# Graph attention turned round: scores with keys on partitions, a multiplied mask, no maximum, and the sum as a 33rd column

## The chip, the cores and the metric

The kernel runs on one core of a Trainium2 chip. The metric is the device time of that core in microseconds (us); lower is better. The kernel before took 2525.3 us, the median of 3 runs (2523.89 to 2526.6).

## The reference

128 graphs of 64 nodes with 256 features go through four layers, each with a layer norm and a ReLU ahead of it and a residual sum behind it. Layers 0 and 1, which the change touches, are attention with 8 heads of 32 features inside each graph. Layer 0 masks by the adjacency, layer 1 adds its logarithm. Layer 2 is a gated graph network with five steps, layer 3 a gated graph convolution. Everything is float32.

```python
# layer 0
q, k, v = split_heads(h @ Wq + bq), split_heads(h @ Wk + bk), split_heads(h @ Wv + bv)
scores = einsum('bhqd,bhkd->bhqk', q, k) / sqrt(HD)
scores = where(adj[:, None] > 0, scores, NEG)
attn = softmax(scores, axis=-1)
out = einsum('bhqk,bhkd->bhqd', attn, v) ... @ Wo + bo
# layer 1
scores = einsum('bhqd,bhkd->bhqk', q, k) / sqrt(HEAD_DIM)
scores = scores + log(adjacency + 1e-06)[:, None]
attn = softmax(scores, axis=-1)
# layer 2: for each of five steps
m = h @ weight[l];  agg = einsum('bij,bid->bjd', A, m);  h = gru_cell(agg, h, ...)
# layer 3
f_hom = norm * (adj @ ((h @ theta) * norm));  f_het = h @ W_h
out = elu(gate * f_hom + (1 - gate) * f_het)          # gate = sigmoid(h @ W_t + b_t)
```

## The kernel before

The program is written out in full, without loops on the chip. Two graphs make a pair of 128 tokens, four pairs a group; there are 16 groups. `attend` works on half a group (two pairs, 256 tokens) in one layer, so it runs 16 x 2 x 2 = 64 times. The order of instructions on each engine is worked out ahead by a planner in the kernel's own Python, which interleaves the groups: while one group is in the five steps of layer 2, the next is in attention and the one before in layer 3. The planner knows costs of operations, among them a cost of changing the shape of the TensorE tiles (full array, 64 by 64, 64 by 32, transposes), and constants such as `FRONT` and `BACK_SPAN` that say how the groups overlap.

The scores come with queries on partitions. DVE scales and biases them, takes the maximum over keys and subtracts it; ACT takes the exponential; DVE sums and inverts; POOL multiplies by the inverse; TensorE turns the weights (`aT`) so that keys lie on partitions; ACT copies them; and in the next call TensorE weighs V.

```python
def scores():                                  # 16 matmuls, tiles of 64 x 64
    for i in range(2):
        for c in range(2):
            for gp in range(2):
                for rh in range(2):
                    ...
                    nc.tensor.matmul(ps[gp * NODES : (gp + 1) * NODES, 2 * c : 2 * c + 2, i, :],
                                     qk[s, c, gp, 0, i * NODES : (i + 1) * NODES],
                                     k_exp[s, c, :, t0 : t0 + NODES], start=True, stop=True)
...
if waiting:                                    # the weighing of the call before, then these scores
    _, weigh_last, reads, po_last, oT_last, finish_last = waiting.pop()
    pe(655, weigh_last, reads, po_last, holds=[oT_last], mode=T32)
    pe(860, scores, [qk, k_exp], pss, holds=es, mode=T64)
    finish_last()
...
for i in range(2):                             # the softmax, twice 128 x 512
    vec(...)   # L767 scalar_tensor_tensor: e = ps * scale + bias
    vec(...)   # L772 tensor_reduce max
    vec2(...)  # L774 e - max
    sca(...)   # L776 exp
    vec(...)   # L777 tensor_reduce sum
    vec(...)   # L779 reciprocal
    pool(...)  # L780 e * (1 / sum)
    def turn(e=e, pa=pa):
        for h in range(4):
            nc.tensor.transpose(pa[:, h * P : (h + 1) * P], e[:, h, :], ident.tile)   # L786
    pe(437, turn, [e, ident], [pa], holds=[aT], mode=TURN)
    sca(...)   # L790 aT <- pa
...
def weigh():                                   # 32 matmuls, tiles of 64 x 32, 64 columns moving
    ...
    nc.tensor.matmul(o[q * HD : (q + 1) * HD, c, s], v[rows, gp, h * HD : (h + 1) * HD],
                     aTs[q // 2][rows, 2 * c + q % 2, s], start=True, stop=True)     # L805

def finish():
    # L813: two copies of 128 x 256, oT <- po;  L818: four matmuls y = oT @ Wo;  L821: x = y + x
    ...

CHANGE = ((0, 95, 95, 0), (250, 30, 135, 200), (237, 135, 30, 187), (0, 95, 95, 0))  # ns, planner
```

Of the kernel before, what the change touches and what calls it, by code (L numbers as in the profile page):

```python
# [11 lines left out]
ALU = mybir.AluOpType  # L12
# [47 lines left out]
FRONT = 0.1  # L60
FRONT_LAST = 0.25
FRONT_SPAN = 0.95
BACK = -0.1
BACK_LAST = 0.35
BACK_SPAN = 0.65
STEP = 0.0
STEP_LAST = -0.1
STEP_SPAN = 0.5
LOCK = 0.3
BACK_END = 0.1  # L70
ENTRY = -0.05
FIRST = -1.2
FIRST_SPAN = 1.2
ORDER = (0, 0, 1, 0, 1, 0)
FUSE = -1.1
FUSE_SPAN = 0.25

# [192 lines left out]

@with_exitstack
def gnn_stack_kernel(ctx: ExitStack, tc: tile.TileContext, a: dict, out: bass.AP):
    nc = tc.nc
    x, adj, nodemask = a["x"], a["adj"], a["nodemask"]
# [95 lines left out]
    with plan.strand(-3.0, 0.1):  # L370


        few = new("few", [P, 7 + PAIRS], 1)

        def fill(n, key, value, rows=slice(0, P)):
            pool(60, lambda: nc.gpsimd.memset(few[rows, n], value), [], [(few, key)])

        fill(slice(0, 1), 0, 1e-6)
        fill(slice(1, 1 + PAIRS), 1, -0.5)
        parity, k_bias = PAIRS + 1, PAIRS + 3  # L380
        fill(slice(parity, parity + 2), 2, 0.0)
        for q in range(4):
            fill(slice(parity + q % 2, parity + q % 2 + 1), 2, 1.0, slice(q * HD, (q + 1) * HD))
        ident = new("ident", [P, P], 1)
        pool(600, lambda: make_identity(nc, ident.tile), [], [ident])

        warm = bank("warm")

        def turn_ident():
            for _ in range(20):  # L390
                nc.tensor.transpose(warm[:, :P], ident.tile, ident.tile)

        pe(4000, turn_ident, [ident], [warm])


        n_rows = 18 + n_pairs
        rows = new("f", [n_rows, P], 1, "rows")

        def fill_rows():
            r0 = 0  # L400
            for name in ("L0_gnn_bq", "L0_gnn_bk", "L2_gnn_b_ih", "L2_gnn_b_hh", "L0_gnn_bv"):
                n = a[name].shape[0] // P
                nc.scalar.dma_start(rows.tile[r0 : r0 + n, :], a[name].rearrange("(r p) -> r p", p=P))
                r0 += n
            nc.scalar.dma_start(rows.tile[r0 : r0 + n_pairs, :],
                                nodemask.rearrange("(t a) n -> t (a n)", a=2))

        plan.add("ACT", 2600, fill_rows, [], [rows], lat=6200)
        load_x(0)

        first = [new("h", [P, 2, 2, D], 4, f"w_{n}") for n in ("qk0", "qk1", "v")]

        def load_first(layer, i):
            t, j = (first[layer], i) if i < 2 else (first[2], layer)
            dma(256, lambda: nc.sync.dma_start(
                t[:, j], a[f"L{layer}_gnn_W{'qkv'[i]}"].rearrange("(c p) o -> p c o", p=P)), [], [(t, j)])
            return t, j

        of_first = [[load_first(0, i) for i in range(2)], []]
        load_adj(0)  # L420

        gw = []

        def load_gw(l):
            t = new(("sg", "sg", "sn", "sn", "Th")[l], [P, 2, D], 2 if l < 4 else 1, f"gw_{l}")
            dma(256, lambda: nc.sync.dma_start(
                t.tile, a["L2_gnn_weight"][l].rearrange("(c p) e -> p c e", p=P)), [], [t])
            gw.append(t)

        load_gw(0)  # L430
        of_first[0].append(load_first(0, 2))
        w_ih = []
        for c, tag in enumerate(("ht", "agg")):
            t = new(tag, [P, 3 * D], 2 if tag == "ht" else 1, f"w_ih{c}")
            dma(384, lambda c=c, t=t: nc.sync.dma_start(
                t.tile, a["L2_gnn_w_ih"][c * P : (c + 1) * P, :]), [], [t])
            w_ih.append(t)
        attn = [(load_w("L0_gnn_Wo", D), load_row("L0_gnn_bo"))]
        for l in range(1, LAYERS):
            load_gw(l)  # L440
        load_x(1)
        of_first[1] = [load_first(1, i) for i in range(3)]
        attn.append((load_w("L1_gnn_Wo", D), load_row("L1_gnn_bo")))
        w_hh = new("w_hh", [P, 3, 7, P], 1)

        def load_hh():
            for c in range(2):
                nc.sync.dma_start(
                    w_hh[:, :, 2 * c : 2 * c + 2, :],
                    a["L2_gnn_w_hh"][c * P : (c + 1) * P, :].rearrange("p (g o q) -> p g o q", g=3, o=2))  # L450

        dma(768, load_hh, [], [w_hh])
# [13 lines left out]
    with plan.strand(-0.9, 0.1):  # L466

        w_o, bo = attn[0]
        bvb = new("aT", [P, 4, P], 2, "bvb")
        pbo = bank("bvo")  # L470
        for c in range(2):
            vec(200, lambda c=c: nc.vector.tensor_copy(
                bvb[:, c, :], cols[:, 16 + c : 17 + c].to_broadcast([P, P])), [cols], [(bvb, c)])
            pe(mm(256), lambda c=c, w_o=w_o: nc.tensor.matmul(
                pbo[:, :D], bvb[:, c, :], w_o[:, c, :], start=c == 0, stop=c == 1),
                [(bvb, c), w_o], [pbo])
        vec(dve(256), lambda bo=bo: nc.vector.tensor_tensor(bo.tile, pbo[:, :D], bo.tile, op=ALU.add),
            [pbo, bo], [bo])
# [25 lines left out]
    def power(dst, src, at, eps, n, name):  # L504

        s = new("pw", [P, n], 3, f"pw_{name}")
        vec2(70, lambda: nc.vector.tensor_scalar(s.tile, at(), eps, None, op0=ALU.add), [src], [s])  # L507
# [27 lines left out]
    def norm_relu_t(xt, half, dst, access, writes, name, by_token=None, by_graph=False):  # L535

        st = new("st", [P, 2, 6], 3, f"st_{name}")
        mv = new("mv", [P, 2, 2], 3, f"mv_{name}")
        rstd = new("rstd", [P, 2], 3, f"rstd_{name}")
        for i in range(2):  # L540
            p = 2 * half + i
            vec(332, lambda p=p, i=i: nc.vector.bn_stats(st[:, i, :], xt[:, p, :]), [(xt, p)], [(st, i)])
            vec(83, lambda i=i: nc.vector.bn_aggr(mv[:, i, :], st[:, i, :]), [(st, i)], [(mv, i)])
        power(rstd, mv, lambda: mv[:, :, 1], EPS, 2, name)
        xn = new("xn", [P, 2, D], 1, f"xn_{name}")
        for i in range(2):
            p = 2 * half + i
            vec2(325, lambda p=p, i=i: nc.vector.tensor_scalar(
                xn[:, i, :], xt[:, p, :], mv[:, i, 0:1], rstd[:, i : i + 1],
                op0=ALU.subtract, op1=ALU.mult), [(xt, p), mv, rstd], [(xn, i)])  # L550
# [53 lines left out]
    def attend(layer, xt, half, bias, bias_at, name, plain):  # L604
# [9 lines left out]
        v = new("v", [P, 2, D], 2, f"v_{name}")  # L614
# [15 lines left out]
        def plainly():  # L630
# [22 lines left out]
            for gp in range(2):  # L653
# [4 lines left out]
            sca(act(512), lambda: nc.scalar.activation(  # L658
                v.tile, pv.tile.rearrange("p (g f) -> p g f", g=2), AF.Copy), [pv], [v])

        def by_seven():
# [38 lines left out]
            def total(bk, t, c, gp):  # L700
# [3 lines left out]
                    v[:, gp, c * P : (c + 1) * P], bk[:, 2 * P : 3 * P], t[:, 2, :], op=ALU.add),  # L704
# [21 lines left out]
            sca(act(128), lambda: nc.scalar.activation(v[:, 0, P:], pb[:, 2 * P : 3 * P], AF.Copy), [pb], [(v, (1, 0))])  # L726
# [9 lines left out]
        def scores():  # L736
# [4 lines that stand above are left out]
# [3 lines left out]
                            nc.tensor.matmul(ps[gp * NODES : (gp + 1) * NODES, 2 * c : 2 * c + 2, i, :],  # L744
# [4 lines left out]
        es = [new("e", [P, 4, 2 * NODES], 3, f"e_{name}_{i}") for i in range(2)]  # L749
        if waiting:  # L750
            _, weigh_last, reads, po_last, oT_last, finish_last = waiting.pop()
            pe(655, weigh_last, reads, po_last, holds=[oT_last], mode=T32)
# [8 lines left out]
        aTs = []  # L761
        shape = [P, HEADS, NODES]
        for i in range(2):
            ps, e = pss[i], es[i]
            m = new("smax", [P, HEADS], 3, f"smax_{name}_{i}")
# [31 lines left out]
        def weigh():  # L797
            for gp in range(2):
                s = slice(gp * NODES, (gp + 1) * NODES)
                for c in range(2):  # L800
                    for q in range(4):
                        for i in range(2):
                            rows, h = slice(i * NODES, (i + 1) * NODES), 4 * c + q
                            o = po[i][:, :D].rearrange("p (c t) -> p c t", c=2)
# [4 lines left out]
        oT = new("oT", [P, 2, 2, P], 1, f"oT_{name}")  # L809

        def finish():
            for i in range(2):
                vec(dve(256), lambda i=i: nc.vector.tensor_copy(  # L813
                    oT[:, i], po[i][:, :D].rearrange("p (c t) -> p c t", c=2)), [po[i]], [(oT, i)])
            py = bank(f"y_{name}")
            for i in range(2):
# [4 lines left out]
            vec(dve(512), lambda: nc.vector.tensor_tensor(  # L821
                xt[:, pp : pp + 2, :], py.tile.rearrange("p (t d) -> p t d", t=2), xt[:, pp : pp + 2, :],
                op=ALU.add), [py, (xt, pp), (xt, pp + 1)], [(xt, pp), (xt, pp + 1)])

        waiting.append((xt, weigh, [v, *aTs], po, oT, finish))

    def flush(xt):
# [4 lines left out]
        pe(655, weigh, reads, po, holds=[oT], mode=T32)  # L832
# [321 lines left out]
    def front(g):  # L1154

        if g % ADJ_GROUPS == 0 and (g // ADJ_GROUPS + 1) * ADJ_GROUPS < n_groups:
# [5 lines left out]
        neg = new("neg", [P, PAIRS, NODES], 1, f"neg_{g}")  # L1162
        vec2(200, lambda: nc.vector.tensor_scalar(
            neg.tile, adjq[:, sel, :], 0.0, NEG, op0=ALU.is_le, op1=ALU.mult), [adjq], [neg])
        for layer in range(2):
            if layer and not g % ADJ_GROUPS:
                log_adj(g // ADJ_GROUPS)
            ladj = adj_vals[g // ADJ_GROUPS][1]
            for half in range(2):
                bias = ladj if layer else neg  # L1170
# [18 lines left out]
        power(norm, deg, lambda: deg.tile, 1e-6, PAIRS, f"deg_{g}")  # L1189
# [15 lines left out]
    def entry(g, xt):  # L1205
# [3 lines left out]
        for half in range(2):  # L1209
            norm_relu_t(xt, half, h, lambda half=half: h[:, :, half * HALF : (half + 1) * HALF],  # L1210
                        [(h, (0, half)), (h, (1, half))], f"{g}_2_{half}", ht)
# [162 lines left out]
    for at, g, l in events:  # L1374
# [19 lines left out]
        if l + 1 == LAYERS:  # L1394
            with plan.strand(begin[g] + 2 + BACK + (BACK_LAST if g + 2 == n_groups else BACK_END if last else 0), BACK_SPAN):
                back(g, *held.pop(g))
    plan.run()
# [33 lines left out]
```

## Time and profile before

| | |
|---|---|
| Time | 2525.3 us (3 runs, 2523.89 to 2526.6) |
| Span of the profiled execution | 2523.7 us, 58158 instructions |
| Granted TensorE clock | 0.998 |
| TensorE transposes of the weights (aT) | 512 records |
| TensorE scores / weighing | 2048 / 4096 records |
| DVE steps of the softmax, in groups of 128 | sum over keys 84.3 us, maximum 83.7 us, minus maximum 86.1 us |
| DMA | 188.47 MB, mean 75 GB/s |

The profile is one execution on the chip. A row of its groups of instructions gives line, engine, operation, tiles written and read, shapes and count; after the bar the time in which at least one instruction of the group ran (us) and the mean duration of one (ns); after the second bar the idle time of the engine just before them. Each matmul of float32 leaves two records, each transpose one. PE is TensorE, PEld its weight loads, DVE VectorE, ACT ScalarE, POOL GpSimd. Matmuls are pipelined, so the duration of one record is longer than the time from its start to the next start.

### The profile page before, as it was taken

The numbers are of one execution on the slowest core, as the hardware profiler recorded it, in microseconds if no ns is written. First come the engines' busy times: TensorE is split into PE (matmuls) and PEld (weight loads), VectorE is DVE, ScalarE is ACT, GpSimd is POOL, SyncE is SP. The second block draws the span as 40 slices with busy tenths as digits, with TensorE's granted clock in tenths as the row PEclk, the third lists the DMA queues.
The fourth block names the chain that finished last, engine by engine and source line by source line (L and its number), as shares of the span: only waits on it lengthen the run. The fifth ranks groups of instructions, "written<-read, shape, count | busy, mean of one in ns | idle before, by whom it ended". The sixth has DMA issues, their size and how long they took to land.

```text
span 2523.7 us, 58158 instructions
## 1 busy us (share of the span) xinstructions
PE 2501.1 (99%) x23511; PEld 2150.9 (85%) x23511; DVE 2038.7 (81%) x4632; ACT 1394.8 (55%) x2806; POOL 879.7 (35%) x892
## 2 busy tenths in 40 slices
PE   9999999999999999999999999999999999999998
PEld 7788888888888888888888888888888888888885
DVE  7886787887878888798877978878788887887667
ACT  4456555555556555565555655556555555555444
POOL 5632323424333333333423334243333333333121
PEclk9999999999999999999999999999999999999999
DMA  6511212113121122222113121131211222211120
GB/s 198 174 67 61 93 49 79 62 54 106 51 99 64 61 75 71 79 71 73 59 68 101 50 84 65 52 101 52 98 64 64 68 71 79 71 49 67 49 71 18
DMA packets 78256, 188.47 MB, mean 75 GB/s; under 512 B 14802, under 2 KB 66852, under 8 KB 67108
## 3 DMA queue, kind: packets, MB, share of 16 engines
q1 hardware_dynamic: 77872, 184.71, 21.8%
q8 instruction: 186, 3.05, 0.5%
q14 instruction: 82, 0.67, 0.1%
q10 hardware_dynamic: 116, 0.04, 0.0%
HBM read 166.70 MB, written 18.02 MB: 73 GB/s over the span
## 4 chain that ended last, share of the span: by engine, by line
PE 96%; DVE 3%; ACT 0%; issue 0%; POOL 0%; DMA 0%; DVEq 0%; POOLq 0%; ACTq 0%
PE gb L932 22%; PE gc L932 17%; PE nb L932 11%; PE nc L932 8%; PE qkvb L682 6%; PE qkvc L682 5%; PE y L818 4%; PE agg L972 3%; PE l3b L1254 3%; PE s L744 3%; PE lnT L522 2%; PE l3c L1254 2%; PE aT L786 2%; PE hT L522 2%; PE o L805 2%; PE hom L1321 1%
## 5 line engine op out<-in xcount | busy, mean ns | idle before, releaser
L1041 POOL TENSOR_TENSOR sn<-h,sn 128x512 f32<-128x512 f32 x158 | 209.1, 1327 | 464.1 <-ACT sn L1039 463.7
L508 POOL TENSOR_TENSOR rstd<-pw,few 128x2 f32<-128x2 f32 x128 | 101.6, 794 | 482.9 <-DVE pw L507 459.7
L780 POOL TENSOR_TENSOR e<-e,ssum 128x512 f32<-128x512 f32 x128 | 149.4, 1175 | 315.9 <-DVE ssum L779 284.5
L932 PE MATMUL gb<-Th,w_hh 128*128 128x256 f32 x960 | 248.1, 381 | 0.0
L932 PE MATMUL gb<-Ta,gv 128*128 128x256 f32 x960 | 246.5, 379 | 0.0
L901 POOL TENSOR_TENSOR Th<-h 128x256 f32<-128x256 f32 x160 | 129.5, 829 | 249.6 <-PE nb L932 177.0
L932 PEld LDWEIGHTS gb<-Th,w_hh 128*128 128x128 f32 x960 | 178.1, 190 | 28.6 <-POOL Th L901 0.4
L932 PEld LDWEIGHTS gb<-Ta,gv 128*128 128x128 f32 x960 | 179.6, 190 | 25.3
L1039 ACT ACTIVATE sn<-sn,b_n 128x512 f32<-128x512 f32 x158 | 114.2, 724 | 123.4 <-DVE sn L1037 121.6
L932 PE MATMUL gc<-h,w_hh 128*128 128x256 f32 x640 | 166.1, 382 | 0.1
L932 PE MATMUL gc<-agg,gv 128*128 128x256 f32 x640 | 165.6, 381 | 0.0
L1043 DVE SCALAR_TENSOR_TENSOR sn<-sg,sn 128x512 f32<-128x512 f32 x158 | 107.4, 686 | 58.5 <-POOL sn L1041 58.3
L1024 ACT ACTIVATE sg<-sg,b_rz 128x512 f32<-128x512 f32 x158 | 105.5, 714 | 78.5 <-DVE sg L1004 78.5
L932 PE MATMUL nb<-Th,w_hh 128*128 128x256 f32 x480 | 144.1, 382 | 0.0
L932 PE MATMUL nb<-Ta,gv 128*128 128x256 f32 x480 | 143.0, 380 | 0.0
L901 POOL TENSOR_TENSOR Th<-h,Th 128x256 f32<-128x256 f32 x160 | 139.1, 869 | 10.4 <-DVE h L1045 4.6
L818 PE MATMUL y<-w_L_gnn_Wo,oT 128*128 128x256 f32 x512 | 138.9, 382 | 0.0
L1035 DVE SCALAR_TENSOR_TENSOR sn<-sg,sn 128x512 f32<-128x512 f32 x158 | 110.4, 700 | 34.8 <-ACT sn L1146 31.7
L985 DVE TENSOR_TENSOR Ta<-agg 128x256 f32<-128x256 f32 x160 | 92.3, 588 | 51.5 <-PE nb L932 41.2
L932 PEld LDWEIGHTS gc<-agg,gv 128*128 128x128 f32 x640 | 118.4, 190 | 16.9 <-issue 2.5
L996 ACT ACTIVATE p5g<-gc 128x512 f32<-128x512 f32 x79 | 46.9, 594 | 149.5 <-PE gc L932 149.4
L932 PEld LDWEIGHTS gc<-h,w_hh 128*128 128x128 f32 x640 | 116.3, 190 | 15.5 <-ACT sg L1031 0.5
(224 smaller groups left out, 6943.4 us busy)
## 6 DMA issues: line engine op xcount, KB each, us to landing
gv<-gates SPq DMA_DIRECT2D x80, 1344.0 KB, 6.0
qw<-kept SPq DMA_DIRECT2D x203, 192.0 KB, 2.4
x<-in_x_dram SPq DMA_DIRECT2D x32, 256.0 KB, 5.5
out_dram<-x SPq DMA_DIRECT2D x32, 256.0 KB, 2.3
gates<-gv SPq DMA_DIRECT2D x5, 1344.0 KB, 5.3
adjq<-in_adj_dram SPq DMA_DIRECT2D x8, 256.0 KB, 4.2
gw<-in_L_gnn_weight_dram SPq DMA_DIRECT2D x5, 256.0 KB, 6.4
kept<-s SPq DMA_DIRECT2D x8, 128.0 KB, 3.5
```

Of the source, the lines that this page charges most:

```text
L508: pool(660 if n == 2 else 970, lambda: nc.gpsimd.tensor_tensor(dst.tile, s.tile, few[:, 1 : 1 + n], op=ALU.pow), [s, (few, 1)], [dst], port=2)
L682: nc.tensor.matmul(bk[:, j * P : (j + 1) * P], lhs, rhs, start=first and j == 0, stop=True, skip_group_check=True)
L780: pool(1000, lambda e8=e8, z=z: nc.gpsimd.tensor_tensor(e8(), e8(), z[:, :, None].to_broadcast(shape), op=ALU.mult), [e, z], [e])
L818: pe(mm(256), lambda i=i, c=c: nc.tensor.matmul(py[:, i * D : (i + 1) * D], oT[:, i, c, :], w_o[:, c, :], start=c == 0, stop=c == 1), [(oT ...
L901: pool(690, lambda: nc.gpsimd.tensor_tensor(T[:, i, :], x(), y(), op=ALU.subtract), reads, [(T, i)])
L932: nc.tensor.matmul(bank_[:, col * HALF : (col + 1) * HALF], at(g, n), rhs(), start=first and j == 0, stop=True, skip_group_check=True)
L1024: sca(act(TOK, 1.5), lambda k=k, col=col: nc.scalar.activation(g_v[:, :, k, :], g_v[:, :, k, :], AF.Tanh, bias=b_rz[:, col : col + 1], sca ...
L1035: vec2(dve(TOK), lambda: nc.vector.scalar_tensor_tensor(a_(), r(), 1.0, a_(), op0=ALU.add, op1=ALU.mult), [*ts[0], n_v], [n_v])
L1039: sca(act(TOK, 1.5), lambda: nc.scalar.activation(a_(), a_(), AF.Tanh, bias=b_n[:, oc : oc + 1]), [n_v, b_n], [n_v])
L1041: pool(1230, lambda: nc.gpsimd.tensor_tensor(b_(), hh(), a_(), op=ALU.subtract), [*hp, n_v], [n_v])
L1043: vec2(dve(TOK), lambda: nc.vector.scalar_tensor_tensor(b_(), z(), 1.0, b_(), op0=ALU.add, op1=ALU.mult), [*ts[1], n_v], [n_v])
L1254: pe(mm(384), lambda: nc.tensor.matmul(bk[:, : 3 * P], b(), w3[:, :, n, :], start=first, stop=True, skip_group_check=True), [w3, *reads], ...
```

## The change

In layers 0 and 1 the roles of queries and keys in the scores are swapped: keys lie on partitions, queries run along the free axis. The result of the exponential is then already laid out as the weighing wants it, and the transposes of the weights go. The maximum is left out. The mask (layer 0: adjacency above zero; layer 1: adjacency + 1e-6, which replaces the added logarithm) is multiplied after the exponential, by POOL; it is turned once a group by two transposes. V gets a 33rd column of a constant for every head, so that the weighing gives the sum of the weights beside the weighted values. The weighing now puts queries on partitions (tiles of 64 by 64, 33 columns moving), DVE divides by the sum, four transposes a call turn the result for the product with Wo. Powers of two (2^32, 2^-42, 2^52, 2^-94) keep the numbers in range.

Without a maximum the exponential can overflow. So the kernel adds up, at the end of this lean network, whether all means that enter layer 2 are finite numbers; if not, a branch runs the whole network once more in the old, general way. Constants of the planner are set anew.

```diff
-FRONT_SPAN = 0.95
+FRONT_SPAN = 0.9
-BACK_SPAN = 0.65
+BACK_SPAN = 0.6
-FIRST = -1.2
-FIRST_SPAN = 1.2
+FIRST = -1.3
+FIRST_SPAN = 1.1
 ... (FRONT, FRONT_LAST, STEP_LAST, BACK_END, FUSE moved likewise)
+WEIGH = (655, 900)
+MASK_UP = 2.0 ** 32
+SUM_DOWN = 2.0 ** -42
+WEIGH_UP = 2.0 ** 52
+Y_DOWN = 2.0 ** -94
 ...
+def gnn_stack_kernel(tc, a, out):
+    with tc.tile_pool(name="flag", bufs=1) as keep:
+        flag = keep.tile([P, 1], mybir.dt.int32, name="flag")
+        network(tc, a, out, flag)
+        beyond = nc.values_load(flag[0:1, 0:1])
+        with tc.If(beyond > 0, preferred_fallthrough_block=False):
+            network(tc, a, out, None)
 ...
-        v = new("v", [P, 2, D], 2, f"v_{name}")
+        v = new("v", [P, 2, HEADS, HD + 1] if lean else [P, 2, D], 2, f"v_{name}")
+        if lean:
+            pool(100, lambda: nc.gpsimd.memset(v[:, :, :, HD:], SUM_DOWN), [], [(v, "one")])
 ...
-            pe(655, weigh_last, reads, po_last, holds=[oT_last], mode=T32)
+            pe(WEIGH[lean], weigh_last, reads, po_last, holds=oT_last, mode=T64 if lean else T32)
 ...
+            if lean:
+                sca(act(512, 0.5), lambda ps=ps, e=e: nc.scalar.activation(
+                    e.tile, ps.tile.rearrange("p (h k) -> p h k", h=4), AF.Exp, scale=scale), [ps], [e])
+                pool(1000, lambda e=e: nc.gpsimd.tensor_tensor(
+                    e.tile, e.tile, bias_at(pp)[:, None, :].to_broadcast([P, 4, 2 * NODES]), op=ALU.mult),
+                    [e, bias], [e])
+                continue
 ...
+                            if lean:
+                                at = (4 * gp + q) * (HD + 1)
+                                nc.tensor.matmul(po[i][c * NODES : (c + 1) * NODES, at : at + HD + 1],
+                                                 aTs[q // 2][rows, 2 * c + q % 2, s], v[rows, gp, h, :],
+                                                 start=True, stop=True)
+                                continue
 ...
+        def divide():
+            for i in range(2):
+                rz = new("rz", [P, HEADS], 2, f"rz_{name}_{i}")
+                o = lambda i=i: po[i][:, : HEADS * (HD + 1)].rearrange("p (h d) -> p h d", d=HD + 1)
+                vec(109, ... nc.vector.reciprocal(rz[:, :, None], o()[:, :, HD:]), [po[i]], [rz])
+                vec(dve(256), ... nc.vector.scalar_tensor_tensor(
+                    os[i].tile, rz[:, :, None].to_broadcast([P, HEADS, HD]), WEIGH_UP, o()[:, :, :HD],
+                    op0=ALU.mult, op1=ALU.mult), [po[i], rz], [os[i]])
+            ... # four transposes of os into one bank, two ACT copies of 128 x 256 into oT
 ...
+            masks = [new(f"mask{layer}", [P, PAIRS, NODES], 2, f"mask{layer}_{g}") for layer in range(2)]
+            ... # two transposes of the adjacency, two DVE passes of 128 x 256: is_gt 0 or + 1e-6, times MASK_UP
 ...
+    if lean:
+        ... # five small instructions: means * 0, their sum, == 0, a 1 x 1 matmul that counts rows, != 128 -> flag
```

## The prediction

> **What bounds the kernel now.** I read the page of the profile first, its busy times and then its chain of work.
>
> ```profile
> PE 2501.1 (99%) x23511; PEld 2150.9 (85%) x23511; DVE 2038.7 (81%) x4632; ACT 1394.8 (55%) x2806; POOL 879.7 (35%) x892
> ...
> PE 96%; DVE 3%; ACT 0%; issue 0%; POOL 0%; DMA 0%; DVEq 0%; POOLq 0%; ACTq 0%
> ```
>
> TensorE (PE) is busy for 99% of the span and makes 96% of the chain that ended last; VectorE (DVE), which the change relieves most, makes 3%. As ends of matmuls are modelled, "busy" alone proves little, so I next read the view of waits for TensorE alone (who waited for whom: us in total, times, longest).
>
> ```profile
> PE gb L932 <- ACT agg L978: 2.4, 3, 1.2
> PE lnT L522 <- DVE xn L548: 1.8, 3, 0.9
> PE aT L786 <- POOL e L780: 1.7, 1, 1.7
> ```
>
> These are the three largest of fourteen rows, which add up to 14.9 us. Cut into three stages, the span has TensorE busy for 122.47 of the first 130 us, 2218.71 of the 2220 us up to 2350 us, and 159.95 of the last 173.7 us. So for 88% of the time TensorE waits for nothing, and the change is worth what it takes from TensorE's own list, plus a few us at the two ends. I then read the groups of instructions of TensorE that the change touches (busy us, mean ns of one | idle before).
>
> ```profile
> L972 PE MATMUL agg<-A,ht 64*64 64x64 f32 x5120 | 92.5, 221 | 0.0
> ...
> L786 PE MATMUL aT<-ident,e 128*128 128x128 f32 x512 | 76.9, 273 | 1.8 <-POOL e L780 1.7
> ...
> L744 PE MATMUL s<-kexp,qk 64*64 64x128 f32 x2048 | 71.0, 275 | 0.0
> ...
> L805 PE MATMUL o<-aT,v 64*32 64x64 f32 x4096 | 55.3, 224 | 0.0
> ```
>
> aT are the transposes of the softmax weights, s the scores, o the weighing by V (tiles of 64 rows by 32 columns), agg the graph sums of layer 2, which already use the tile shape that the new weighing will have (64 by 64). A matmul leaves two records, a transpose one. Durations overlap, so costs must come from one start to the next, in the timeline of TensorE (start us, us, what, records).
>
> ```profile
> 1011.24 1.03 PE L932 MATMUL gc<-h,w_hh 128*128 128x256 f32 x4
> 1012.19 0.86 PE L805 MATMUL o<-aT,v 64*32 64x64 f32 x64
> 1012.98 1.12 PE L744 MATMUL s<-kexp,qk 64*64 64x128 f32 x32
> 1014.03 1.13 PE L932 MATMUL gc<-agg,gv 128*128 128x256 f32 x4
> 1015.00 0.59 PE L818 MATMUL y<-w_L_gnn_Wo,oT 128*128 128x256 f32 x2
> ...
> 1022.43 1.16 PE L972 MATMUL agg<-A,ht 64*64 64x64 f32 x64
> 1023.52 1.13 PE L932 MATMUL gb<-Th,w_hh 128*128 128x256 f32 x4
> ...
> 1028.37 0.60 PE L786 MATMUL aT<-ident,e 128*128 128x128 f32 x4
> 1028.81 0.60 PE L522 MATMUL hT<-ident,h 128*128 128x128 f32 x4
> ```
>
> ```profile
> 1074.14 1.10 PE L744 MATMUL s<-kexp,qk 64*64 64x128 f32 x32
> 1075.07 1.11 PE L972 MATMUL agg<-A,ht 64*64 64x64 f32 x64
> 1076.11 1.13 PE L932 MATMUL gb<-h,w_hh 128*128 128x256 f32 x4
> ```
>
> Four transposes take 1028.81 - 1028.37 = 0.44 us, 0.11 each. One weighing takes 0.79 us ahead of scores, scores 1.05 us ahead of full-array work, agg 1.09. Where scores are followed by agg, both 64 by 64, they take 0.93 and agg 1.04: 0.12 and 0.05 less. Four full-array records take 0.86 in a stream (1019.32 to 1020.18 in the same view), but 0.95 before small tiles and 0.97 after: each change of tile shape is paid for.
>
> [...] mean load 135 ns for agg, 105 ns for o. [...] No run here shows a branch.
>
> **The change, part by part, on TensorE.** `attend` runs 16 groups x 2 layers x 2 halves = 64 times.
> - Removed: 8 transposes aT a call, 512 x 0.11 = 56.3 us.
> - Added: 4 transposes a call of the weighed result by query, 256 x 0.11 = 28.2 us; 2 a group to turn the adjacency, 32 x 0.11 = 3.5 us.
> - Weighing: still 32 matmuls, 64 records, but stationary is now a 64 x 64 block of the weights and V moves with 33 columns. Only 4 tiles run side by side instead of 8, so 8 rounds instead of 4. The measured twin is agg: also 64 records in tiles of 64 by 64, 64 columns moving. With a neighbour of its own shape, agg + scores cost 0.93 + 1.04 = 1.97 us; the old o + s cost 0.79 + 1.05 = 1.84. That is +0.13 us a call if 33 columns are no faster than 64. [...] I take off 0.03 and settle on +0.10 us. 64 x 0.10 = +6.4 us. Some agg next to o no longer change shape: agg followed directly by o at 1045.71 shows 1.09 us today and would be about 0.98; a dozen such places make -1.3 us.
> - One more matmul and the scores with roles swapped (keys stationary, queries moving): same count and shape, 0.
>
> Sum on TensorE: -56.3 + 28.2 + 3.5 + 6.4 - 1.3 = **-19.5 us**.
>
> **Beside it, off the path.** DVE loses the biased copy, maximum, subtraction, sum, reciprocal and the copy of o: 82.6 + 83.7 + 86.1 + 84.3 + 24.6 + 50.0, and the mask's 4.6, together 416 us in its groups. It gains 128 reciprocals (0.19 us, L779) and 128 scaled products of 256 from PSUM (0.47 us, L1324) and 32 masks (0.42 us), about 98 us. DVE goes from 2039 to about 1720 us busy. ScalarE (ACT) loses the 75.2 us of aT copies and the logarithms with their table loads (about 16 us) and gains 128 copies of 256 (0.38 us, L695), 49 us. GpSimd (POOL) keeps 128 products of 512, now by the mask. None of it stands in the chain between 130 and 2350 us, so I give it nothing there. The softmax's way from scores to weighing loses four DVE passes of 0.67 us, transposes and a copy, a good 4 us; the way from weighing to y gains a reciprocal, a product, transposes and a copy, about 2 us. That matters only in the first 130 us, where 7.5 us are idle, 1.4 before the first instruction: the 1.73 us for aT at 52.95 goes, and some of the rest. I give -3 us, the retuned order included. The last 174 us hold the last layers' products, hardly any attention: 0.
>
> **The branch.** Every engine loads a flag and compares. The flag is made by five small instructions that depend on the last entry into layer 2, long before the end. The last SyncE issue is at 2520.53 us, the span ends at 2523.7. The load and the branch come after that issue or beside its flight[...]. I give +3 us, the least founded term.
>
> Sum: 2525.3 - 19.5 - 3 + 3 = 2505.8. Since a full list rarely yields every us taken out (the order shifts, small waits appear as TensorE gets ahead of DVE in layer 2), I give 2 back: **2508 us**, -0.7%.
>
> **Rivals.** (a) The weighing costs much more than its twin, for instance because rows of 33 or the 33rd column break the overlap of loads: at 1.3 us a call it is +0.3 to +0.4, +22 us, and the time is 2522. For it: 8 rounds, twice the present number. Against: agg has the same 8. (b) The branch costs a fetch on every engine in turn or waits for the output to land: +10 to +15 us, and the time is 2518. Nothing in this profile speaks to it. (c) DVE was the hidden limit, and 320 us less of it frees the kernel: then 2450 or less. For it: 81% busy; against: 41.2 us of its idle time before the differences Ta alone end on TensorE, and there are only 1.3 us of idle TensorE in 2220. (d) The new way exp, GpSimd, weighing makes TensorE wait: GpSimd is 35% busy and its product takes 1.18 us, and the weighing stands a whole call later in the order; 1 us in every tenth call would be 6 us, 2514.
>
> **Range and chances.** Weighing between -5 and +15 us of its term, branch 0 to +10, waits -7 to +5: 8 in 10 for 2498 to 2520. Faster by over 2% means under 2474.8, which needs (c): 0.02. Slower by over 2% means over 2575.8, which needs the general way to run as well or a large stall: 0.015. Within 2%: 0.965.
>
> **What would show it.** Right: no aT group, 256 transposes more for the result, TensorE at 99%, its idle before o near 0, o from start to start at 0.9 to 1.0 us ahead of s, s after it near 1.0, DVE near 1720 us. Wrong: o above 1.2 us (a), a stretch without work after the last store (b), a TensorE waiting for GpSimd's e or for the new division (d), or full-array matmuls themselves closer together (c).

## The result and the profile after

The changed kernel takes 2550.9 us (median of 4 runs, 2549.27 to 2551.98) against 2525.85 us for the kernel before beside it: a ratio of 1.0101, 95% interval 1.0087 to 1.0116. It is 25 us slower, where I had predicted 17 us faster, with a range up to 2520.

The page of the changed kernel, its busy times and its chain:

```profile
PE 2519.4 (99%) x23289; PEld 2174.6 (85%) x23289; DVE 1743.4 (68%) x4140; ACT 1337.7 (52%) x2782; POOL 857.6 (34%) x957
...
PE 97%; DVE 1%; ACT 1%; issue 0%; DMA 0%; POOL 0%; DVEq 0%; ACTq 0%; POOLq 0%
```

DVE fell by 295 us, TensorE is still the whole chain, and it is busy for longer although it has 222 records fewer in each row. So TensorE's own work grew. Its groups that the change touches (the line numbers moved: L1057 is agg, L787 scores, L856 weighing, L882 the new transposes of the result, L1254 those of the adjacency):

```profile
L787 PE MATMUL s<-kexp,qk 64*64 64x128 f32 x2048 | 101.7, 275 | 0.4 <-ACT kexp L662 0.3
L1057 PE MATMUL agg<-A,ht 64*64 64x64 f32 x5120 | 97.6, 222 | 0.0
L856 PE MATMUL o<-v,e 64*64 64x33 f32 x4096 | 73.2, 220 | 5.2 <-issue 5.2
L882 PE MATMUL oT<-ident,os 128*128 128x128 f32 x256 | 38.7, 274 | 0.0
L1254 PE MATMUL mask<-ident,adjq 128*128 128x128 f32 x32 | 7.0, 303 | 0.0
```

The transposes aT are gone, as meant. The surprise is the first row: the scores, which I had left at a difference of 0, stand at 101.7 us of busy time against 71.0, with the same 2048 records of the same mean of 275 ns. As many records of the same duration that cover more time must overlap less. The timeline of TensorE in the changed kernel shows it:

```profile
1163.86 1.14 PE L856 MATMUL o<-v,e 64*64 64x33 f32 x64
1164.82 1.57 PE L787 MATMUL s<-kexp,qk 64*64 64x128 f32 x32
1166.32 1.13 PE L1017 MATMUL gb<-agg,gv 128*128 128x256 f32 x4
```

The weighing takes 1164.82 - 1163.86 = 0.96 us to the start of the scores, close to its predicted price; the scores take 1.50 us instead of about 1.03.

The reason stands in one line of the change that the diff above, an excerpt, does not show. The loops around the score matmul stayed as they were, and only the place of its output moved (`...` marks lines left out):

```diff
             for i in range(2):
                 for c in range(2):
                     for gp in range(2):
                         for rh in range(2):
                             ...
-                            nc.tensor.matmul(ps[gp * NODES : (gp + 1) * NODES, 2 * c : 2 * c + 2, i, :],
+                            to, at = (i, gp) if lean else (gp, i)
+                            nc.tensor.matmul(ps[to * NODES : (to + 1) * NODES, 2 * c : 2 * c + 2, at, :],
```

A score matmul has a tile of 64 by 64 where full-array work has 128 by 128 (`64*64` and `128*128` in the rows above), a quarter. I read the half of the partitions that it writes as the column half of its tile, and `rh`, the half of the partitions that it reads, as the row half; the times of e1, e2 and e11 below fit this reading. Before, the output half was `gp`, so `gp` and `rh` sent four matmuls in a row to four tiles. Now it is `i`, the outermost loop: eight matmuls in a row share two tiles, then eight the other two.

### The profile page after: what moved, and what is told of

Read it like the earlier page. It is cut to its first block, busy times and chain, and to the rows that moved or that the text cites. A ratio compares the mean times of both kernels' runs of the same rounds, so it can differ in the third digit from the quotient of the medians.

```text
span 2550.1 us, 57184 instructions
## 1 busy us (share of the span) xinstructions
PE 2519.4 (99%) x23289; PEld 2174.6 (85%) x23289; DVE 1743.4 (68%) x4140; ACT 1337.7 (52%) x2782; POOL 857.6 (34%) x957
## 3 DMA queue, kind: packets, MB, share of 16 engines
q8 instruction: 186, 3.05, 0.5%
## 4 chain that ended last, share of the span: by engine, by line
PE 97%; DVE 1%; ACT 1%; issue 0%; DMA 0%; POOL 0%; DVEq 0%; ACTq 0%; POOLq 0%
PE gb L1017 22%; PE gc L1017 16%; PE nb L1017 11%; PE nc L1017 8%; PE qkvb L724 6%; PE qkvc L724 5%; PE y L902 4%; PE s L787 4%; PE agg L1057 3%; PE l3b L1362 3%; PE o L856 2%; PE lnT L545 2%; PE hT L545 2%; PE l3c L1362 2%; PE hom L1429 1%; PE oT L882 1%
## 5 line engine op out<-in xcount | busy, mean ns | idle before, releaser
L1126 POOL TENSOR_TENSOR sn<-h,sn 128x512 f32<-128x512 f32 x158 | 200.6, 1273 | 430.5 <-ACT sn L1124 430.4
L811 POOL TENSOR_TENSOR e<-e,mask 128x512 f32<-128x512 f32 x128 | 161.5, 1281 | 200.2 <-ACT e L809 200.2
L986 POOL TENSOR_TENSOR Th<-h 128x256 f32<-128x256 f32 x160 | 114.7, 737 | 263.0 <-PE nb L1017 172.2
L1070 DVE TENSOR_TENSOR Ta<-agg 128x256 f32<-128x256 f32 x160 | 85.5, 553 | 87.5 <-PE nb L1017 53.4
L1017 PEld LDWEIGHTS gc<-agg,gv 128*128 128x128 f32 x640 | 121.5, 190 | 16.4 <-issue 0.2
L902 PE MATMUL y<-w_L_gnn_Wo,oT 128*128 128x256 f32 x512 | 133.2, 380 | 0.0
L809 ACT ACTIVATE e<-s 128x512 f32<-128x512 f32 x128 | 69.5, 595 | 107.1 <-PE s L787 107.0
L1120 DVE SCALAR_TENSOR_TENSOR sn<-sg,sn 128x512 f32<-128x512 f32 x158 | 115.4, 737 | 11.8 <-ACT sn L1231 5.4
```

The source lines that it names most:

```text
L811: pool(1000, lambda e=e: nc.gpsimd.tensor_tensor(e.tile, e.tile, bias_at(pp)[:, None, :].to_broadcast([P, 4, 2 * NODES]), op=ALU.mult), [e ...
L902: pe(mm(256), lambda i=i, c=c: nc.tensor.matmul(py[:, i * D : (i + 1) * D], oT[:, i, c, :], w_o[:, c, :], start=c == 0, stop=c == 1), [(oT ...
L986: pool(690, lambda: nc.gpsimd.tensor_tensor(T[:, i, :], x(), y(), op=ALU.subtract), reads, [(T, i)])
L1017: nc.tensor.matmul(bank_[:, col * HALF : (col + 1) * HALF], at(g, n), rhs(), start=first and j == 0, stop=True, skip_group_check=True)
L1120: vec2(dve(TOK), lambda: nc.vector.scalar_tensor_tensor(a_(), r(), 1.0, a_(), op0=ALU.add, op1=ALU.mult), [*ts[0], n_v], [n_v])
L1126: pool(1230, lambda: nc.gpsimd.tensor_tensor(b_(), hh(), a_(), op=ALU.subtract), [*hp, n_v], [n_v])
```

## The experiments

Beside each time stand the ratio to the kernel before, run next to it, and its 95% interval. Theory A: this order of tiles costs 0.47 us in each of 64 calls, 30 us. Rival B: the swap of keys and queries as such, or the weighing's new shape next to it, makes the scores slow. Four kernels tell them apart, and measure the branch.

**e1**, the changed kernel with its score loops nested anew:

```diff
-            for i in range(2):
+            for gp in range(2):
                 for c in range(2):
-                    for gp in range(2):
+                    for i in range(2):
                         for rh in range(2):
```

> The changed kernel with one edit: the four loops of the scores nested so that the index of the output half (keys' half i, the column of the tile) and the head half rh (the row of the tile) are innermost, so that four matmuls in a row go to four different tiles. Theory A (order of tiles): scores fall from 1.50 to about 1.03 us from start to start, 64 x 0.47 = 30 us, so 2521 us (2517 to 2526). Theory B (the swap of keys and queries itself, or the neighbour of the same tile shape, makes the scores slow): scores stay near 1.50 us and the time at 2551 us.

Measured: 2519.99 us (ratio to before 0.9981, 0.9974 to 0.9988). From the same place in the program:

```profile
1147.75 1.14 PE L856 MATMUL o<-v,e 64*64 64x33 f32 x64
1148.71 1.08 PE L787 MATMUL s<-kexp,qk 64*64 64x128 f32 x32
1149.72 1.13 PE L1017 MATMUL gb<-agg,gv 128*128 128x256 f32 x4
```

The scores are back at 1149.72 - 1148.71 = 1.01 us, the weighing is unchanged at 0.96.

The starts of the single records show how. Take the 18 calls of each trace whose scores stand between full-array work. In e1 their 32 records start in eight groups of four, the first group at 0 and the last at 0.82 us. In the changed kernel they start in twos: eight pairs from 0 to 0.82 us, and eight more from 0.50 to 1.32 us. The records do not name their tile, but fours against twos fit four tiles at work against two, and the 0.50 us by which the second eight pairs lag are the loss.

**e2**, the kernel before with only its loops nested the wrong way, `for gp`, `for i`, `for c`, `for rh`:

> The kernel before with one edit: the same 16 score matmuls, but with the index of the output half (graph gp, the column of the tile) outermost, as the changed kernel has it in effect. Nothing else of the change. Theory A: scores rise from 1.03 to about 1.50 us, 64 x 0.47 = 30 us, so 2555 us (2549 to 2560). Theory B: 2525 us, no difference.

Measured: 2556.62 us (1.0123, 1.0106 to 1.0139).

```profile
1025.22 0.86 PE L805 MATMUL o<-aT,v 64*32 64x64 f32 x64
1026.01 1.59 PE L744 MATMUL s<-kexp,qk 64*64 64x128 f32 x32
1027.53 1.13 PE L932 MATMUL gc<-agg,gv 128*128 128x256 f32 x4
```

With no swap and the old weighing (0.79 us), the scores take 1.52 us, and their records start in the same twos. The order of tiles alone does it, in either kernel: 31 us each way. B falls.

**e3**, the changed kernel without the branch:

```diff
         network(tc, a, out, flag)
-        beyond = nc.values_load(flag[0:1, 0:1])
-        with tc.If(beyond > 0, preferred_fallthrough_block=False):
-            network(tc, a, out, None)
```

> The changed kernel without the load of the flag, the branch and the general network behind it (the guard against overflow is left out; the flag is still computed). From the last trace the end after the last store is 8.1 us against 3.2 us before: 2546 us (2544 to 2548). If the branch cost nothing that lies on the path: 2551 us. If the doubled program also slowed the middle, for instance by fetches of instructions: below 2543 us.

Measured: 2546.29 us (1.0081, 1.0065 to 1.0098). The branch costs 4.6 us. It lies at the end: from the last issue of an output to the end of the span it is 3.3 us here, against 8.1.

**e4**, e1 and e3 together:

> Both edits, order of the score tiles and no branch (the guard left out). If the two add up: 2551 - 30 - 5 = 2516 us (2512 to 2521). If Theory B holds: 2546 us.

Measured: 2515.39 us (0.9960, 0.9948 to 0.9973). The two add up. But 2515 is still more than the 2505 that my sum gives without a branch. The waits of TensorE in e1 name a candidate, which the kernel before does not have:

```profile
PE o L856 <- issue: 5.3, 6, 1.2
...
PE hom L1429 <- issue: 1.3, 1, 1.3
...
PE gb L1017 <- issue: 0.7, 1, 0.7
```

"Issue" is a wait for nothing that the profile shows. In the changed kernel it stands in the middle of one weighing, where all operands had been waited for already:

```profile
1007.95 0.90 PE L856 MATMUL o<-v,e 64*64 64x33 f32 x46
1009.33 0.47 PE L856 MATMUL o<-v,e 64*64 64x33 f32 x17 [0.48 <-issue]
```

I numbered TensorE's instructions in the trace in order of start, weight loads, matmuls and semaphores together. A gap is the time from one start to the next. In the changed kernel 42 gaps of over 0.38 us lie between 130 and 2350 us. Of these, 31 are of 0.41 to 0.50 us and leave many different remainders when the number of the instruction behind them is divided by 256, none more than twice. The other eleven, of 0.70 to 1.40 us, all leave 193. The DMA records show a 16 KiB block of instructions moved ahead of the end of each of them, begun 2.2 to 2.7 us and landed 1.2 to 1.6 us before the gap ends (in the changed kernel and in e1).

Theory C: a block of 256 instructions arrives too late when the work ahead of it is used up fast; the weighing and a graph sum are such work, 128 instructions in each and 2 us for both. Rival D: something in the weighing after a graph sum stalls by itself, wherever it stands. The page of the changed kernel has the size of a block: 3.05 MB in 186 packets, 16.4 KB each.

```profile
q8 instruction: 186, 3.05, 0.5%
```

**e5**, e1 with every later TensorE instruction 24 places earlier:

```diff
-            for _ in range(20):
+            for _ in range(8):
                 nc.tensor.transpose(warm[:, :P], ident.tile, ident.tile)
```

> The changed kernel with reordered scores, and 8 instead of 20 warming transposes at the start, so that every later TensorE instruction stands 24 places earlier in its stream. Theory C (blocks of 256 instructions are fetched late): the eleven stalls of 0.4 to 1.7 us in the middle, about 11 us in all, all stand at the same place modulo 256, so most of them go or move: about 4 us left of them, 2513 us (2510 to 2517). Theory D (the stall belongs to the weighing next to the graph sums, whatever its place): they stay where they are, 2520 us.

Measured: 2516.37 us (0.9965, 0.9953 to 0.9978). **e6** has 32 there:

> The same with 32 warming transposes: every later TensorE instruction 24 places later[...]. Theory C: about 3 us of stalls left, 2513 us (2510 to 2518). Theory D: 2521 us.

Measured: 2516.43 us (0.9962, 0.9948 to 0.9976). **e10** has 1:

> The changed kernel with reordered scores and 1 warming transpose instead of 20: TensorE instructions 38 places earlier. With 24 places earlier the stalls that were left, five of 0.5 to 1.1 us, still stood at the same place modulo 256, inside the weighing next to the graph sums, and were about a third shorter. Theory C: they get shorter again or go, 2514 us (2512 to 2518)[...]. Theory D: 2516 to 2520 us with stalls at the same weighings and of the same size.

Measured: 2516.68 us (0.9963, 0.9951 to 0.9976). Counted in the traces, gaps of over 0.38 us ahead of a number that leaves 193, between 130 and 2350 us:

```text
                      number   sum us   what stands behind them
before                     0      0.0
changed                   11     11.2   o (7), hom (2), hom to gb, gb
e1                        10     12.2   the same weighings and their neighbours
e5 (24 earlier)            5      4.5   o
e6 (24 later)              6      6.9   o
e10 (38 earlier)           7      6.1   o, then s, and one gb of 1.8
e7 (planner, below)        2      1.8   o
```

With every shift the gaps stay at 193 modulo 256 and change the instruction they hit; in e10 five of them stand at the scores instead of the weighing. So they belong to the place in the stream and not to the operation: D falls, and C holds as far as a late block goes. Its second half, that fast work makes the block late, is too simple. In the changed kernel 22 other block ends have as fast work ahead of them (the last 128 instructions in under 1.25 us) and none stalls; there the last transfer of a block had begun at least 5.9 us earlier. Why it began so late at the eleven stalls stays open.

The sizes I expected were too hopeful: half of the stalls went, not most, and a shift of 38 was no better than one of 24. Nor did the time fall by what the stalls lost. From e1 to e5 the gaps fell by 7.7 us, the two profiled executions differ by 6.5 us and the medians by 3.6. Between the two traces the stretch from 130 to 2350 us became 6.6 us shorter, but the first 20 us were 1.9 us longer in e5. They were 2.0 us longer in e4 too, with the same twenty warming transposes as e1, so that part need not come from the shift.

**e7**, e1 with the planner's bonus for neighbours in small tiles at zero:

```diff
-BESIDE = 0.45
+BESIDE = 0.0
```

> The changed kernel with reordered scores, and the planner's bonus for putting work in small tiles next to other such work set to zero (BESIDE = 0). Graph sums followed directly by a weighing get fewer, so fewer stretches with 256 instructions in 2 us. Theory C and D: the stalls of 11 us mostly go, but some 30 changes of tile shape at 0.1 to 0.2 us come back, 3 to 5 us: 2514 us (2509 to 2520). If clustering is worth more than its stalls: above 2521 us.

Measured: 2537.94 us (1.0048, 1.0032 to 1.0065). The 2514 us were a miss, and the other forecast, above 2521 us, held: the stalls at block ends went down to 1.8 us, but the small-tile work now lies in 203 separate stretches instead of 135, and the time rose by 18 us. At 0.2 us for the two edges of each of 68 further stretches, an estimate from the timeline before (four full-array records take 0.86 us in a stream, 0.95 and 0.97 next to small tiles), the changes of shape come to 14 us; with the 10 us of stalls saved, some 15 us more are lost elsewhere, and that was not taken apart.

**e8**, e1 with the nine planner constants of the kernel before:

> The changed kernel with reordered scores and the planner's nine constants (FRONT to FUSE) of the kernel before. If the constants were a gain of their own: 2523 to 2530 us. If they only move the order about: 2517 to 2523 us, with stalls at other places.

Measured: 2529.49 us (1.0014, 1.0007 to 1.0021). Its waits of TensorE begin with

```profile
PE lnT L545 <- DVE xn L575: 8.4, 13, 0.9
```

so the new constants were a gain of 9.5 us in this kernel: without them TensorE waits for the norm's output once in nearly every group. Its trace has no gap at 193 at all, where e1 has 12.2 us of them. So the old constants lose some 21 us in other ways; the row above is 8.4 of them, the rest was not taken apart.

**e11**, the changed kernel with the loops `c`, `i`, `gp`, `rh`: the output half changes after every fourth matmul.

> The changed kernel with the scores nested so that the column half changes after every fourth matmul (two matmuls for each of two tiles, then the other two tiles), with branch and 20 warming transposes. If TensorE can start a matmul on a free tile past one or two that wait for a busy tile: about 1.15 to 1.3 us for the scores from start to start, 2530 to 2538 us. If it can't look past a waiting one at all: as bad as the changed kernel, 1.5 us and 2551 us. If four matmuls in order are as good as strict turns: 1.03 us and 2520 us.

Measured: 2522.96 us, a single run without an interval.

```profile
1132.26 1.15 PE L787 MATMUL s<-kexp,qk 64*64 64x128 f32 x32
1133.35 1.13 PE L1017 MATMUL gb<-h,w_hh 128*128 128x256 f32 x4
```

1.09 us (the same at 18 places between full-array work), against 1.03 in strict turns (1034 ns at 18 places of e1). That is nearest to the third forecast. The starts show four records at a time for the first five groups, then twos: the second pair of records begins 0.03 us after the first, and the second series is not 0.50 us late. Four matmuls in one output half before the other half gets its own are nearly free (1.09 us against 1.03); eight are not (1.52).

**e9**, e5 with the other layout of the branch, `preferred_fallthrough_block=True`:

> The changed kernel with reordered scores and 8 warming transposes, and the branch told to prefer the other layout (preferred_fallthrough_block=True). In the last traces SyncE stands still for 2.9 us between its jump and its next instruction. If the layout decides on that jump: 2513.5 us (2.9 less than 2516.4). If one jump remains in either layout: 2516.4 us (2514 to 2518).

Measured: 2514.06 us (0.9953, 0.9936 to 0.9969), 2.3 us less than e5. **e12**, e5 without the branch, the guard left out:

> The changed kernel with reordered scores, 8 warming transposes and no branch (the guard against overflow left out). If the three causes add up: 2516.4 - 4.6 = 2511.8 us (2509 to 2515).

Measured: 2510.3 us (0.9938, 0.9921 to 0.9954). So e9 is the best version that keeps the guard, 11.6 us under the kernel before and 36.8 under the change as it was made (measured in another batch of runs).

## Why the prediction was wrong

The start-to-start times of all TensorE records, added up by group over the whole trace, give the account (us; the prediction as a difference from before):

```text
                         predicted        before    changed   e12
aT                         -56.3            56.7       0        0
result turned (oT)         +28.2             0        28.2     28.3
adjacency turned            +3.5             0         4.4      4.3
scores + weighing + agg     +5.1           205.6     251.8    217.7
after the last issue        +3               3.2       8.1      3.3
```

- **The step that failed** is "the scores with roles swapped (keys stationary, queries moving): same count and shape, 0". Count and shape were right; the price is not made of them alone: records that start in fours make 1.03 us of the scores, records in twos 1.52. For the weighing I counted tiles side by side, and the traces fit that count: the first 32 records of a weighing before start in four groups of eight within 0.24 us, while all 64 of a new one start in sixteen groups of four, 58 ns apart from the second group on. I did not ask it of the scores, whose loop order gave them two tiles at a time instead of four. e1 and e2 measure it: 31 us, which alone turns the predicted gain into a loss. The order itself could be read from the diff before any run.
- The transposes came as predicted: 56.7 us out, 28.2 and 4.4 in.
- The weighing's twin gave the right price ahead of scores: predicted at 0.9 to 1.0 us, 0.95 measured (954 ns at the median of 32 places of e1); agg ahead of a weighing 0.98, as predicted. There are 27 such places and not a dozen, since the planner now knows the shapes as equal. But the other 32 weighings stand ahead of full-array work, at 1.02 to 1.07 us against 0.79 before, and I had priced all 64 like those ahead of scores. In e12 scores, weighing and agg together grew by 12.1 us, 8.2 without its 3.9 us of stalls, where I had +5.1. The 0.03 us a call that I took off for the shorter stream was my estimate; between full-array work the weighing takes 0.026 us less than agg (1.066 us against 1.092), with mean loads as long as agg's (135 and 134 ns in the changed kernel). Rival (a), above 1.2 us, is out.
- "small waits appear" was not what happened: between 130 and 2350 us TensorE's waits for other engines came to 1.7 us, against 1.0 before, and none was of a weighing for GpSimd, which puts rival (d) out. What appeared were stalls at the ends of blocks of instructions, 11 us in the changed kernel, a term that my sum lacked. The kernel before had 0.0 us of them; the changed kernel had them at eleven block ends, where the transfer began 2.2 to 2.7 us before TensorE went on.
- The branch was 4.6 us (e3) against +3, inside its range. In the trace's records of the changed kernel SyncE loads the flag for 0.50 us at 2542.43, compares at 2543.00 (0.05 us), waits for the output until 2544.91 (its last packet ends at 2544.42), jumps at 2545.53 and has its next instruction at 2548.46. In the other layout (e9) it compares at 2508.24 and goes on at 2511.09, so that one standstill of 2.85 us covers both the jump and the landing of the output. Whether the standstill at the jump is a fetch of instructions was not shown: two blocks of 8 KiB of instructions are moved within it, begun at 2546.39 and 2546.72 in the changed kernel, but the records do not say for which engine, and no run took a fetch by itself.
- The waits at the start were predicted at -3. In the first 130 us TensorE is busy for 125.44 us instead of 122.47, which fits; but slower scores and warming transposes count as busy too, and how much of it was useful work was not taken apart.
- DVE at 1743 us against "about 1720", and worth nothing, as said: rival (c) is out by the same run. Rival (b) had the right sign and a third of the size.

With the loops in order, the shift and no branch, e12 stands at 2510.3; my sum without the branch is 2505.8 - 3 = 2503, or 2505 with the 2 us given back. Of the 5 to 7.5 us between, 3.9 us are the stalls that e12 still has, counted as above, and about 3 the weighing that I priced too low (8.2 - 5.1). So little stays open.

## What to carry to other kernels

When a change moves where a small-tile matmul reads or writes, list the tile of each matmul in program order again. Here the output half had to come round within a few matmuls: against a change after every second, a change after every fourth cost 0.06 us a call, after the eighth 0.49. The scores' price of 1.03 us held only for the order it was measured in. The count of records and their mean duration (2048 of 275 ns in both kernels) did not show the loss; the busy time of the group (101.7 us against 71.0) and the start-to-start times did. In a program like this one, without loops and with a full engine, look for waits that name nothing, and count the instructions modulo the size of a block, 256 in these traces.

## What the runs showed of the hardware

- Sixteen float32 matmuls of 64 x 64 with 128 columns moving, between full-array work, take 1.03 us when the half of the partitions that they write changes after every second (e1), 1.09 when it changes after every fourth (e11) and 1.52 when it changes after the eighth (the changed kernel), each at 18 places. The last is less than twice the first: its second series of records begins at 0.50 us, while the first runs on to 0.82.
- With 33 columns moving the weighing takes 1.066 us (5 places of e1), agg with 64 takes 1.092 (39 places), both between full-array work. Here, with 64 stationary columns, the shorter stream saved 26 ns.
- In the changed kernel TensorE stalled eleven times for 0.70 to 1.40 us ahead of instructions whose numbers all leave 193 modulo 256; the last block of instructions had begun to move 2.2 to 2.7 us before each stall's end. At 22 other block ends work of up to 140 instructions per us (128 in 0.91 us) passed without a stall; there the block had begun to move at least 5.9 us earlier. With the stream 24 instructions earlier the kernel took 3.6 us less (e5 2516.37 us, e1 2519.99).
- Eight warming transposes at the start (2516.37 us), or one (2516.68), came within 0.3 us of thirty-two (2516.43), and the mean granted clock of the profiled execution was 0.998 in each.
